# Graph attention on one core: the scores of heads 0 and 1 in one two-bank PSUM tile with one exponential, in place of two one-bank tiles with one exponential each

## The chip, the core and the metric

The kernel runs on one core of a Trainium2 chip. The metric is the device time of one execution in microseconds (us); three runs of the kernel before are given, and one further execution was recorded by the profiler. The engines are named as in the profile: PE is TensorE (PEld its weight loads), DVE is VectorE, ACT is ScalarE, POOL is GpSimd, SP is SyncE, which issues the DMAs. PSUM is the memory that PE writes into; in this kernel it is used as eight banks of 512 float32 columns on 128 partitions.

## What is computed

Two layers of graph attention over 3327 nodes of 128 features. Layer 0 is one softmax over masked cosine scores, a weighted sum, a residual and a layer norm. Layer 1 takes nearly all the time:

```python
q = (x @ Wq.T).reshape(d, n, h)      # d = 128 heads, h = 8 features each
k = (x @ Wk.T).reshape(d, n, h)
v = (x @ Wv.T).reshape(d, n, h)
a = jnp.einsum('dnh,dmh->dnm', q, k) * scale
a = a + spatial_encoding + edge_encoding     # both are adj, so a + 2 adj
a = jax.nn.softmax(a, axis=2)
out = jnp.einsum('dnm,dmh->dnh', a, v)
```

So there are 128 heads of 8 features, each with a full 3327 by 3327 score matrix and a full softmax with its row maximum. A last projection, a residual and a layer norm follow.

## The kernel before, in words

The first two stages (layer 0, and the projections with their transposes to DRAM) end at about 1740 us of the profile. The change lies in the third stage, the attention of layer 1, which runs from there to about 16380 us. The final projection follows.

**Units.** The work of the attention is cut into units of four heads and one block of queries. There are nine blocks: eight of three tiles (384 queries), and a last one of two tiles (256 queries). With 32 groups of four heads this makes 288 units, 256 of 384 queries and 32 of 256. A unit runs over 26 tiles of 128 keys, and each of these is a *step*: 7488 steps in all, 6656 with 384 query columns and 832 with 256.

**What a step does.** The order of the instructions on PE, ACT, DVE and POOL is the order in which the loop at L705 writes them (`manual_schedule`); nothing reorders them. In each step, in this order:

1. PE writes the shift (the negative row maximum, in three bf16 parts) of heads 2 and 3 into the tile `eb`, which has two banks (`shifts`, L592).
2. PE makes the score products for a *later* unit's row maxima, and DVE reduces them (`max_pair`: two heads in two banks, reduced at L515 or L526; `max_single`: one head in one bank, reduced at L536 or L540; the products are L500). A step has one pair and one single. One of them stands here, the other at point 5. When the pair is of heads 0 and 1 it comes here, else the single does. Both have a single buffer, so the products of a step wait for DVE's reduction of the same kind of the step before. In the last block only every second step has a pair.
3. PE adds the scores of heads 2 and 3 to `eb` (`scores`, L598). ACT takes the exponential of both heads from the two banks in one instruction (L724) into `pb`, and POOL multiplies `pb` with the exponential of twice the adjacency (L725).
4. PE writes the shift of heads 0 and 1 into two tiles `ea` of one bank each (L592).
5. PE makes the other of the two products for the row maxima.
6. PE adds the scores of heads 0 and 1 (L598), and then twice the adjacency (`add_adj`, L579): four matmuls for head 0, then four for head 1, on four groups of 32 output columns.
7. ACT takes the exponentials of `ea`, one instruction for head 0 and one for head 1 (L754), into the two halves of `pa`.
8. PE multiplies the `pa` and `pb` of two steps earlier with the values and adds to `acc` (`weigh`, L609).

In some steps of each unit there is more: at key tiles 22 to 24 (of 26) PE turns the next unit's shift in the unused columns 384 to 511 of head 0's `ea` bank and ACT copies it out (L565, L745); at key tile 20 the same place takes the finished output of the unit before (L627, L639); at key tile 1 ACT copies `acc` (L620).

**PSUM.** The eight banks are all used: two by `ea` (a pool of two one-bank buffers), two by `eb`, two by the pair of row-maximum products, one by the single, one by `acc`. Each step therefore takes the same two `ea` buffers, and the shift of a head in the next step waits for the exponential that read that head's buffer.

Of the kernel before, what the change touches and what calls it, by code (L numbers as in the profile page):

```python
# [9 lines left out]
F32 = mybir.dt.float32  # L10
F32R = mybir.dt.float32r
BF16 = mybir.dt.bfloat16
AF = mybir.ActivationFunctionType
ALU = mybir.AluOpType
AX = mybir.AxisListType
PSUM = bass.MemoryType.PSUM
DRAM = bass.MemoryType.DRAM

P = 128
# [26 lines left out]
def gnn_two_layers(  # L46
# [11 lines left out]
    nc = tc.nc  # L58
# [328 lines left out]
    with ExitStack() as at:  # L387
# [1 line left out]
        keys = at.enter_context(tc.tile_pool(name="at_k", bufs=3))  # L389
        pp = at.enter_context(tc.tile_pool(name="at_p", bufs=4))  # L390
        sm = at.enter_context(tc.tile_pool(name="at_sm", bufs=2))
        ps_a = at.enter_context(tc.tile_pool(name="at_a", bufs=2, space=PSUM))
        ps_b = at.enter_context(tc.tile_pool(name="at_b", bufs=1, space=PSUM))
        ps_m = at.enter_context(tc.tile_pool(name="at_m", bufs=1, space=PSUM))
        ps_o = at.enter_context(tc.tile_pool(name="at_o", bufs=1, space=PSUM))
# [29 lines left out]
        def load_adj_tile(b, j):  # L425
            w = width(b)
            nc.sync.dma_start(aT[:, j, :w], aT_s[b][:, j, :w])

        def exp_adj_tile(b, j):
            w = width(b)  # L430
            nc.scalar.activation(eT[:, j, :w], aT[:, j, :w], AF.Exp, scale=2.0)
# [4 lines left out]
        def load_unit(i):  # L436
            b, g = units[i]
            u = Unit()
            u.i, u.b, u.g = i, b, g
            u.nq = width(b)  # L440
            u.nt = u.nq // P

            u.kx = keys.tile([P, NP], F32R, name="kx")
            u.qx = keys.tile([P, QB], F32R, name="qx")
            kx, qx = u.kx.bitcast(F32), u.qx.bitcast(F32)
            for c in range(2):
                nc.sync.dma_start(
                    kx.rearrange("(y c) n -> c y n", c=2)[c],
                    kp_s[4 * g : 4 * g + 4].rearrange("d f r n -> (d f r) n"),
                )  # L450
                for r in range(2):
                    nc.sync.dma_start(
                        qx.rearrange("(y r c) n -> r c y n", r=2, c=2)[r, c, :, : u.nq],
                        qp_s[4 * g : 4 * g + 4, :, c, b * QB : b * QB + u.nq].rearrange(
                            "d f n -> (d f) n"
                        ),
                    )
            u.vt = keys.tile([P, 4, T, H + 1], F32, name="vt")
            nc.sync.dma_start(u.vt, vt_s[g])
            if g % 2 == 0:  # L460
                load_unit.mx = sm.tile([P, 2, 4, QT, 7], F32, name="mx")
            u.mx_both = load_unit.mx
            u.mx = u.mx_both[:, g % 2]
            u.cx = sm.tile([P, QB], BF16, name="cx")
            return u
# [96 lines left out]
        def shift_turn(u, q, dst, start):  # L562
            for h in range(4):
                r = slice(32 * h, 32 * h + 32)
                nc.tensor.matmul(  # L565
                    dst[r],
                    parts[u.i % 2][:, q, h],
                    unit,
                    start=start,
                    stop=True,  # L570
                    tile_position=(0, 32 * h),
                    skip_group_check=True,
                )
# [90 lines left out]
        with tc.manual_schedule(  # L664
            engines={
                mybir.EngineType.PE,
                mybir.EngineType.Activation,
                mybir.EngineType.DVE,
                mybir.EngineType.Pool,
            }  # L670
        ):
            us = {0: load_unit(0), 1: load_unit(1)}
            steps = {}

            def max_step(k):

                i, j = divmod(k, 2 * T)
                if 2 * i >= NU:
                    return None
                if j == 0:  # L680
                    steps[i] = max_steps(2 * i, 2 * i + 1)
                return steps[i][j]

            def new_a():
                return [ps_a.tile([P, 512], F32, name="ea") for _ in range(2)]

            for j in range(T):
                load_adj_tile(0, j)
            for k in range(T + AHEAD):
                pair, single = max_step(k)  # L690
                max_pair(*pair)
                max_single(*single)
                if k == T:
                    shift_parts(us[0])
            e = ps_b.tile([P, 2, 512], F32, name="eb")
            for q in range(QT):
                shift_turn(us[0], q, e[:, 0, q * P : (q + 1) * P], True)
            nc.scalar.copy(us[0].cx, e[:, 0, :QB])
            for j in range(T):
                exp_adj_tile(0, j)  # L700

            todo = []
            turn = []
            done = None
            for s in range(NU * T + LAG):  # L705
                i, j = divmod(s, T)
                u = us.get(i)
                if u is not None:
                    if j == 2 and i + 2 < NU:
                        us[i + 2] = load_unit(i + 2)  # L710
                    k = s + T + AHEAD
                    pair, single = max_step(k) or (None, None)
                    early = pair is not None and pair[1] == (0, 1)

                    e_b = ps_b.tile([P, 2, 512], F32, name="eb")
                    b01 = [e_b[:, x] for x in range(2)]
                    shifts(u, b01, (2, 3))
                    if early:
                        max_pair(*pair)
                    elif single is not None:  # L720
                        max_single(*single)
                    scores(u, j, b01, (2, 3), True)
                    pt_b = pp.tile([P, 2, QB], F32, name="pb")
                    nc.scalar.activation(pt_b[:, :, : u.nq], e_b[:, :, : u.nq], AF.Exp)  # L724
                    nc.gpsimd.tensor_tensor(  # L725
                        pt_b[:, :, : u.nq],
                        pt_b[:, :, : u.nq],
                        eT[:, j, : u.nq].unsqueeze(1).to_broadcast([P, 2, u.nq]),
                        ALU.mult,
                    )  # L730
                    e_a = new_a()
                    shifts(u, e_a, (0, 1))
                    if early:
                        max_single(*single)
                    elif pair is not None:
                        max_pair(*pair)
                    scores(u, j, e_a, (0, 1), False)
                    free = e_a[0][:, QB:]
                    x = us.get(i + 1)
                    copies = []  # L740
                    q = j - (T - 4)
                    if x is not None and 0 <= q < x.nt:
                        shift_turn(x, q, free, False)
                        copies.append(
                            lambda: nc.scalar.copy(x.cx[:, q * P : (q + 1) * P], free)  # L745
                        )
                    if j == T - 6 and done is not None:
                        values_turn(done, free, False)
                        copies.append(lambda: finish(done, free))
                    pt_a = pp.tile([P, 2, QB], F32, name="pa")  # L750
                    for h, e in enumerate(e_a):
                        add_adj(e, u, j)
                    for h, e in enumerate(e_a):
                        nc.scalar.activation(pt_a[:, h, : u.nq], e[:, : u.nq], AF.Exp)  # L754
                    for f in copies:
                        f()
                    todo.append((u, j, (pt_a, pt_b)))

                    if k % (2 * T) in (T, 2 * T - 1):
                        v = us.get(k // (2 * T) * 2 + (k % (2 * T) > T))  # L760
                        if v is not None:
                            shift_parts(v)
                if s >= LAG:
                    w = todo.pop(0)
                    weigh(*w)
                    if w[1] == T - 1:
                        take(w[0])
                        done = us.pop(w[0].i)

                if turn and turn[0][0] <= s:  # L770
                    exp_adj_tile(*turn.pop(0)[1:])
                if u is not None and i + 1 < NU and units[i + 1][0] != u.b:
                    load_adj_tile(u.b + 1, j)
                    turn.append((s + 5, u.b + 1, j))
            e = ps_b.tile([P, 2, 512], F32, name="eb")
            values_turn(done, e[:, 0], True)
            finish(done, e[:, 0])
# [73 lines left out]
```

## Time and profile before

| | |
|---|---|
| three runs, median | 16488.67 us (16487.55 to 16496.15) |
| the profiled execution's own time | 16497.24 us |
| its span, from the first to the last instruction | 16495.5 us |
| attention stage, 384-column units | about 1741 to 15099 us |
| attention stage, 256-column units | about 15099 to 16378 us |
| exponential of heads 2 and 3, 128x768 (L724) | 6656 of 811 ns |
| exponential of head 0 or 1, 128x384 (L754) | 13312 of 490 ns |
| the same with 512 and 256 columns | 832 of 598 ns, 1664 of 383 ns |
| mean granted TensorE clock | 0.971 over the span, 1.00 in the attention |

The profile gives each instruction a start and a duration. In the timeline view a row merges instructions of the same kind that stand next to each other: the first column is the start of the first, the second the time from there to the end of the last, and "x2" how many there are. The text in brackets is the time that the engine sat idle before it, and whom it waited for. Matmuls run in several groups of rows or columns of the array at once, and their ends are modelled. A PE that looks busy throughout may therefore still be waiting in its queue; this is seen only by comparing the start of a matmul with the end of the instruction on another engine that it waits for.

### The profile page before, as it was taken

The page shows a single profiled execution, that of the slowest core. Times are in us where ns is not written, and L with a number is a line of the kernel's source. Part 1 is how long each engine was busy: PE and PEld are TensorE (multiplying, and loading weights), DVE is VectorE, ACT ScalarE, POOL GpSimd, SP SyncE. Part 2 cuts the span into 40 slices and gives each one's busy share as a digit, 9 for nine tenths or more (in the row PEclk, how much of TensorE's full clock was granted, in tenths as well). Part 3 has the DMA queues.
Part 4 walks back from the last instruction along what each step waited for, and adds up shares of the span by engine and source line. Part 5 has one row for each costly group of instructions (what it writes and reads, how often), then busy time and mean ns, then how long its engine had stood idle before and what let it go on. Part 6 is the DMA issues. An engine that isn't in the chain of part 4 may idle for free.

```text
span 16495.5 us, 506265 instructions
## 1 busy us (share of the span) xinstructions
PE 15510.9 (94%) x217532; PEld 6894.2 (42%) x217532; DVE 14320.0 (87%) x16017; ACT 12381.3 (75%) x24535; POOL 14030.4 (85%) x9088
## 2 busy tenths in 40 slices
PE   4462899999999999999999999999999999999999
PEld 3341344444444444444444444444444444444555
DVE  8862899999999999999999999999999999998775
ACT  1220688888888888888888888888888888888776
POOL 3314699999999999999999999999999999999886
PEclk7786899999999999999999999999999999999999
DMA  1127111111111111111111111111111111111112
GB/s 66 63 114 286 65 49 49 49 55 49 49 49 55 48 45 49 55 49 49 49 55 49 49 49 54 45 49 49 55 49 49 49 55 49 49 47 54 65 60 69
DMA packets 415019, 988.86 MB, mean 60 GB/s; under 512 B 192224, under 2 KB 312544, under 8 KB 367200
## 3 DMA queue, kind: packets, MB, share of 16 engines
q1 hardware_dynamic: 412768, 956.46, 17.0%
q8 instruction: 1704, 27.92, 0.7%
q14 instruction: 547, 4.48, 0.1%
HBM read 808.05 MB, written 148.24 MB: 58 GB/s over the span
## 4 chain that ended last, share of the span: by engine, by line
PE 89%; DVE 4%; issue 3%; DMA 2%; POOL 1%; ACT 1%; SPq 0%; DVEq 0%; ACTq 0%; POOLq 0%
PE acc L609 28%; PE ea L579 19%; PE m L500 14%; PE eb L592 12%; PE ea L592 9%; PE ea L598 2%; PE eb L598 2%; DVE mx L515 1%; PE ea L565 1%; DVE s L273 1%; PE av L187 1%; POOL low L359 1%; PE ea L627 1%; DVE mx L536 1%; PE sc L170 0%
## 5 line engine op out<-in xcount | busy, mean ns | idle before, releaser
L725 POOL TENSOR_TENSOR pb<-pb,eT 128x768 f32<-128x768 f32 (+1 forms) x7488 | 13176.2, 1765 | 1102.7 <-ACT pb L724 868.1
L515 DVE TENSOR_REDUCE mx<-m 128x2 f32<-128x1024 f32 x6784 | 8272.9, 1219 | 518.3 <-PE eb L598 277.3
L724 ACT ACTIVATE pb<-eb 128x768 f32<-128x768 f32 (+1 forms) x7488 | 5896.2, 787 | 2506.1 <-PE eb L598 1765.1
L500 PE MATMUL m<-kx,qx 32*128 32x512 f32 (+1 forms) x23296 | 6784.1, 471 | 160.9 <-DMA vt<-vt_s 117.5
L754 ACT ACTIVATE pa<-ea 128x384 f32<-128x384 f32 (+1 forms) x14976 | 6339.6, 478 | 55.2 <-PE ea L579 42.3
L609 PE MATMUL acc<-pb,vt 128*9 128x384 f32 (+1 forms) x29952 | 5903.5, 474 | 0.1
L609 PE MATMUL acc<-pa,vt 128*9 128x384 f32 (+1 forms) x29952 | 5900.7, 474 | 0.0
L536 DVE TENSOR_REDUCE mx<-m 128x1 f32<-128x512 f32 x6400 | 4378.9, 684 | 692.1 <-PE m L500 317.9
L592 PEld LDWEIGHTS <-one 3*128 3x128 bf16 x29952 | 1508.8, 91 | 5565.7 <-issue 4663.3
L579 PE MATMUL ea<-aT,two 128*32 128x384 bf16 (+1 forms) x59904 | 3715.8, 325 | 0.0
L598 PE MATMUL ea<-qx,kx 32*128 32x384 f32 (+1 forms) x14976 | 3444.3, 437 | 0.0
L598 PE MATMUL eb<-qx,kx 32*128 32x384 f32 (+1 forms) x14976 | 3437.2, 451 | 0.0
L592 PE MATMUL ea<-cx,one 3*128 3x384 bf16 (+1 forms) x14976 | 3294.8, 322 | 2.2
L500 PEld LDWEIGHTS m<-kx,qx 32*128 32x128 f32 x23296 | 2815.8, 182 | 525.4 <-issue 117.8
L592 PE MATMUL eb<-cx,one 3*128 3x384 bf16 (+1 forms) x14976 | 2462.4, 326 | 11.1 <-ACT pb L724 10.4
L609 PEld LDWEIGHTS acc<-pa,vt 128*9 128x9 f32 x29952 | 1410.9, 91 | 786.9 <-issue 0.3
L579 PEld LDWEIGHTS <-two 128*32 128x32 bf16 x59904 | 946.2, 95 | 1418.7 <-issue 1278.2
L598 PEld LDWEIGHTS eb<-qx,kx 32*128 32x128 f32 x14976 | 1461.2, 189 | 0.0
L598 PEld LDWEIGHTS ea<-qx,kx 32*128 32x128 f32 x14976 | 1431.2, 182 | 8.4 <-issue 4.5
L609 PEld LDWEIGHTS acc<-pb,vt 128*9 128x9 f32 x29952 | 1417.8, 91 | 0.6 <-POOL pb L725 0.6
L540 DVE TENSOR_REDUCE mx<-m 128x2 f32<-128x512 f32 x1088 | 748.0, 688 | 96.2 <-PE eb L598 44.8
L187 PE MATMUL av<-xs,pt 128*128 128x128 f32 x1352 | 223.4, 330 | 476.2 <-DVE rden L292 310.4
(113 smaller groups left out, 5245.1 us busy)
## 6 DMA issues: line engine op xcount, KB each, us to landing
kx<-kp_s SPq DMA_DIRECT2D x576, 832.0 KB, 4.7
vt<-vt_s SPq DMA_DIRECT2D x288, 468.0 KB, 4.9
qx<-qp_s SPq DMA_DIRECT2D x1024, 48.0 KB, 5.0
raw<-in_adj_dram SPq DMA_DIRECT2D x25, 1663.5 KB, 6.3
aT_s<-aT SPq DMA_DIRECT2D x8, 2496.0 KB, 9.2
aT<-aT_s SPq DMA_DIRECT2D x208, 96.0 KB, 1.9
vt_s<-vals SPq DMA_DIRECT2D x8, 1872.0 KB
q_s<-row SPq DMA_DIRECT2D x26, 512.0 KB, 2.6
```

The costliest lines, as they stand in the source:

```text
L187: nc.tensor.matmul(acc, pt[:, i * P : (i + 1) * P], value(t), start=(t == 0), stop=(t == T - 1))
L500: nc.tensor.matmul(dst, u.qx[rows(a), q * P : (q + 1) * P], u.kx[rows(a), k0:k1], start=True, stop=True,)
L515: nc.vector.tensor_reduce(u.mx[:, h, qs[0], c], m, axis=AX.X, op=ALU.max)
L536: nc.vector.tensor_reduce(u.mx[:, a, qs[0], c : c + 1], m, axis=AX.X, op=ALU.max)
L540: nc.vector.tensor_reduce(u.mx[:, a, qs[0] : qs[1] + 1, c], m.rearrange("p (q k) -> p q k", q=2), axis=AX.X, op=ALU.max,)
L579: nc.tensor.matmul(e[r, : u.nq], two[:, r], aT[:, j, : u.nq], start=False, stop=True, tile_position=(0, 32 * c), skip_group_check=True,)
L592: nc.tensor.matmul(e[:, : u.nq], one[r], u.cx[r, : u.nq], start=True, stop=False, skip_group_check=True)
L598: nc.tensor.matmul(e[:, : u.nq], u.kx[rows(a), j * P : (j + 1) * P], u.qx[rows(a), : u.nq], start=False, stop=stop, skip_group_check=True,)
L609: nc.tensor.matmul(acc[32 * h : 32 * h + H + 1, : u.nq], u.vt[:, h, j], pts[h // 2][:, h % 2, : u.nq], start=(j == 0), stop=(j == T - 1), ...
L724: nc.scalar.activation(pt_b[:, :, : u.nq], e_b[:, :, : u.nq], AF.Exp)
L725: nc.gpsimd.tensor_tensor(pt_b[:, :, : u.nq], pt_b[:, :, : u.nq], eT[:, j, : u.nq].unsqueeze(1).to_broadcast([P, 2, u.nq]), ALU.mult,)
L754: nc.scalar.activation(pt_a[:, h, : u.nq], e[:, : u.nq], AF.Exp)
```

## The change

The pool of `ea` gets one buffer in place of two, and its tile has two banks in place of one. The two heads' score tiles are the two halves of this tile. The two exponentials become one instruction over both halves. `free`, the unused columns of head 0's bank, is in the same place as before. In the built instruction streams the number and the order of all other instructions are the same. On PE the shift of head 0 now waits for the one exponential of the step before, and the shift of head 1, which waited for its own head's, has no wait left; on ACT the one exponential waits for the last of the eight `add_adj` matmuls, where before the first exponential waited for the fourth and the second for the eighth.

```diff
-        ps_a = at.enter_context(tc.tile_pool(name="at_a", bufs=2, space=PSUM))
+        ps_a = at.enter_context(tc.tile_pool(name="at_a", bufs=1, space=PSUM))
...
-            def new_a():
-                return [ps_a.tile([P, 512], F32, name="ea") for _ in range(2)]
-
...
-                    e_a = new_a()
+                    ea = ps_a.tile([P, 2, 512], F32, name="ea")
+                    e_a = [ea[:, x] for x in range(2)]
                     shifts(u, e_a, (0, 1))
...
                     pt_a = pp.tile([P, 2, QB], F32, name="pa")
-                    for h, e in enumerate(e_a):
+                    for e in e_a:
                         add_adj(e, u, j)
-                    for h, e in enumerate(e_a):
-                        nc.scalar.activation(pt_a[:, h, : u.nq], e[:, : u.nq], AF.Exp)
+                    nc.scalar.activation(pt_a[:, :, : u.nq], ea[:, :, : u.nq], AF.Exp)
```

## The prediction

> **What bounds the kernel now.** I read the page first, for the busy shares and the costliest groups, then the timeline of two steady steps of a 384-column unit and of two steps of a 256-column unit, since the page's shares hide which wait ends last.
>
> ```profile
> PE 15510.9 (94%) x217532; PEld 6894.2 (42%) x217532; DVE 14320.0 (87%) x16017; ACT 12381.3 (75%) x24535; POOL 14030.4 (85%) x9088
> ...
> L515 DVE TENSOR_REDUCE mx<-m 128x2 f32<-128x1024 f32 x6784 | 8272.9, 1219 | 518.3 <-PE eb L598 277.3
> ...
> L754 ACT ACTIVATE pa<-ea 128x384 f32<-128x384 f32 (+1 forms) x14976 | 6339.6, 478 | 55.2 <-PE ea L579 42.3
> ```
>
> PE never looks idle and ACT has a quarter of the span free: by these shares alone, shortening ACT is worth nothing. But PE's idleness does not show when its queue waits, so I compare starts with ends. In the timeline of a 384-column unit, two successive steps:
>
> ```profile
> 9072.84 0.87 ACT L754 ACTIVATE pa<-ea 128x384 f32<-128x384 f32 x2
> ...
> 9073.46 0.33 PE L592 MATMUL eb<-cx,one 3*128 3x384 bf16 x2
> ...
> 9073.81 0.34 PE L592 MATMUL ea<-cx,one 3*128 3x384 bf16 x2
> ...
> 9074.01 1.23 DVE L515 TENSOR_REDUCE mx<-m 128x2 f32<-128x1024 f32 x1 [0.24 <-PE eb L598]
> 9074.11 0.81 ACT L724 ACTIVATE pb<-eb 128x768 f32<-128x768 f32 x1 [0.41 <-PE eb L598]
> 9074.26 0.51 PE L579 MATMUL ea<-aT,two 128*32 128x384 bf16 x8
> ...
> 9074.82 0.87 ACT L754 ACTIVATE pa<-ea 128x384 f32<-128x384 f32 x2
> ...
> 9075.15 0.68 DVE L536 TENSOR_REDUCE mx<-m 128x1 f32<-128x512 f32 x1
> ...
> 9075.69 0.37 PE L592 MATMUL ea<-cx,one 3*128 3x384 bf16 x2
> ...
> 9075.89 0.50 PE L500 MATMUL m<-kx,qx 32*128 32x512 f32 x1
> ...
> 9076.32 0.51 PE L579 MATMUL ea<-aT,two 128*32 128x384 bf16 x8
> ...
> 9076.78 0.87 ACT L754 ACTIVATE pa<-ea 128x384 f32<-128x384 f32 x2
> ...
> 9077.41 0.33 PE L592 MATMUL eb<-cx,one 3*128 3x384 bf16 x2
> ```
>
> The two steps take 9077.41 - 9073.46 = 3.95 us, 1.97 each. There is a loop of DVE and PE with just this length. From the shift of `eb` (9073.46) to the pair's reduction (9074.01) is 0.55; pair and single reduce back to back until 9075.15 + 0.68 = 9075.83, 1.82; the next step's single product starts 0.06 later (9075.89), because its only buffer has just come free; adds start 0.43 after it (9076.32); the shift of `eb` two steps on comes 1.09 later. 0.55 + 1.82 + 0.06 + 0.43 + 1.09 = 3.95. **DVE's reductions and the way back through PE set the pace of the 384-column units**, and no exponential is in that loop. Counted over the first 6000 steps of the trace, one of the two products starts 0.06 behind its reduction in 82% of them.
>
> ACT is close behind. Its loop runs through `ea`: shift, adds, exponentials, shift. At 9075.69 the two exponentials end (9074.82 + 0.87), and the row of the `ea` shift that starts there spans 0.37 instead of 0.34, which puts its second matmul some 0.05 after that end: PE waited for ACT. But the single product that follows waits for DVE until 9075.89 anyway, so this wait is covered.
>
> In the 256-column units DVE has half the pairs, and the same comparison gives another bound:
>
> ```profile
> 15505.00 0.28 PE L592 MATMUL eb<-cx,one 3*128 3x256 bf16 x2
> ...
> 15505.83 0.40 PE L579 MATMUL ea<-aT,two 128*32 128x256 bf16 x8
> ...
> 15506.24 0.66 ACT L754 ACTIVATE pa<-ea 128x256 f32<-128x256 f32 x2
> ...
> 15506.60 0.28 PE L592 MATMUL eb<-cx,one 3*128 3x256 bf16 x2
> ...
> 15506.67 0.55 PE L592 MATMUL ea<-cx,one 3*128 3x256 bf16 x2
> ...
> 15507.27 0.40 PE L579 MATMUL ea<-aT,two 128*32 128x256 bf16 x8
> ...
> 15507.73 0.66 ACT L754 ACTIVATE pa<-ea 128x256 f32<-128x256 f32 x2
> ```
>
> The exponentials end at 15506.90; the `ea` row that follows spans 0.55 for two matmuls of some 0.28, so the second starts at about 15506.95, 0.05 after them. Here **ACT's loop through `ea` is the bound**.
>
> **The change part by part.**
>
> *One exponential for two.* Two 128x384 take 0.87 from the first start to the last end; one 128x768 from two banks is L724 as it stands, 0.81. That is 0.06 less ACT time per step, 0.06 x 6656 = 400 us in all, and 0.66 - 0.60 = 0.06 on the 832 small steps. All of it lies beside the DVE loop in the large units, so it is worth nothing as such.
>
> The Trainium skill (ScalarE: Activation LUTs, What ACT_TABLE_LOAD costs) gives an ACTIVATE a fixed 186 ns plus 0.833 ns per column, with 93 ns overlapped back to back. By that rule merging would take 93 ns off each step, 0.70 ms over 7488 steps if ACT set the pace, and the time would be some 15,800 us. The rows above have 0.06, and ACT does not set it.
>
> *The later start.* Before, head 0's exponential starts 0.11 us after its own four adds where nothing else holds it (112 ns is the median of such steps in the trace; in the timeline the first four end at about 9076.32 + 0.34, and 9076.78 follows, when the eight still run until 9076.32 + 0.51 = 9076.83). The merged one needs all eight. No row shows this wait; the nearest is the same 0.11 behind the eighth add. So at the first step shown it starts at 9074.26 + 0.51 + 0.11 = 9074.88 instead of 9074.82 and ends at 9075.69, as now. At the second it starts at 9076.94 instead of 9076.78 and ends at 9077.75 instead of 9077.65: 0.10 later. **The change delays the release of `ea`, although it shortens ACT.** Behind it on PE's queue, everything of the step waits.
>
> The Trainium skill (PSUM — Partial Sum Buffer, Summary: rules for kernel authors) says to aim at a different bank when reading PSUM while matmuls run. That speaks against this change: two separate banks let head 0 be read while head 1 is written, which the 9076.78 row shows for 0.05 us.
>
> *What the delay costs in the large units.* The new loop through `ea` is: shift to adds 0.44 at the least (9073.81 to 9074.26), eight adds 0.51, wait 0.11, exponential 0.81, release 0.05: 1.92. The DVE loop needs 1.97 on average, so 0.05 of slack is left per step. It bites only where steps alternate between short and long, as here: 9075.34 to 9077.41 is 2.07 and the one before 1.88, below 1.92. Since the DVE loop ties each step to the one after the next, the short step can grow to 1.92 and the long one shrink to 2.02 at no cost, except once, when the pattern is entered, about 0.045 us per unit. 256 units x 0.045 = 12 us. Ends: 0 (absorbed in the slower steps at the unit's end) to 0.09 per unit, 23 us.
>
> *What it costs in the small units.* First step: adds end 15506.23, merged start 15506.34, plus 0.60 is 15506.94 against 15506.90: 0.04 to 0.05 later, on the bounding loop. Second step: adds end 15507.67, start 15507.78, end 15508.38 against 15508.39: nothing. 0.049 x 416 pairs of steps = 20 us. Ends: 0, and 0.05 on each of the 832, 42 us.
>
> *The rest.* PE drops one wait per step and head 0's shift waits longer than before; it had been ready 0.4 us before its turn, and the loop above counts it with head 1's. The copies out of `free` (272 ns, 3 per unit) come behind an exponential that ends up to 0.10 later; the next use of ACT is L724, before which ACT now sits idle 0.4 us, and that hides it. `weigh` reads `pa` two steps later. No DMA moves, and SP and POOL get the same instructions in the same order.
>
> **Sum.** 16497.2 (the profiled execution's own time, 1.7 over its span) + 12 + 20 = 16529. That execution lies 8.6 us above the median of the three runs, 16488.7; timed runs should so give 16521, +0.19%.
>
> **Rivals.** (1) *Markedly slower: the loop through `ea` becomes the bound everywhere.* Place: shift, adds, exponential, shift. It has 0.05 us of slack at 1.92; from there each further 0.01 costs up to 0.01 x 6656 = 67 us. If the merged exponential started 0.06 us later than I count (the wait for the eighth add is no row of before), half of it would be eaten by slack: 0.02 x 6656 = 130 on the large units and 0.06 x 832 = 50 on the small ones beyond the forecast, 16,700. For it: matmul ends are modelled. Against: 0.11 holds wherever head 0 waits for its adds. 20%. (2) *Faster: ACT's chain L724, L754, L754 sets the pace.* For it: `ea` follows the exponentials by 0.05 in 30% of those 6000 steps. If it were the bound over two steps, 0.06 per pair of steps comes off: 0.03 x 6656 = 200 us, 16,290. Against: in just those steps the adds end too late for the merged start to gain (9074.88, above). 8%. (3) *Nothing measurable changes*: both delays are absorbed, 16,489, as the small steps' loop finds slack that I do not see. 6%.
>
> **Chances.** Forecast 66%, with its own range 16,490 to 16,555 from the ends above. A measurement of this kernel can tell about 0.2% from no change, which is 16,521.7, so the forecast lies on that line: of its 66 I put 36 within and 30 above. Faster 8, within 36 + 6 = 42, slower 30 + 20 = 50. The range that leaves two in ten out: from 16,475 to 16,650.
>
> **What will show it.** The row of `pa` should be one 128x768 with 0.81, started 0.11 behind the last add; large steps that alternate 1.92 and 2.02 in place of 1.88 and 2.07; single products still 0.06 behind DVE's single. In the small units two steps should take 3.08 in place of 3.03. I am wrong if the single product no longer follows DVE by 0.06 (rival 1: then `ea`'s shift follows the exponential by 0.05 in every step), or if the two-step time of the large units falls below 3.93.

## The result, and the profile after

| | before | changed |
|---|---|---|
| median of the runs | 16488.39 us (16487.55 to 16496.15, 4 runs) | 16630.01 us (16626.7 to 16630.85, 4 runs) |
| span of the profiled execution | 16495.5 us | 16628.2 us |
| 384-column units, from their first step's shift to the first one of the 256-column units | 13358.4 us | 13462.3 us |
| 256-column units, from their first step's shift to their last's | 1278.5 us | 1306.5 us |

The ratio is 1.0084, 95% interval 1.0067 to 1.0102: 142 us slower. Of the 132.7 us between the spans, 103.9 lie in the large units and 28.0 in the small ones; the stages around them differ by 1 us.

The page of the changed kernel, the lines that answer to those shown of before:

```profile
PE 15583.1 (94%) x217532; PEld 6981.7 (42%) x217532; DVE 14314.6 (86%) x16017; ACT 12396.5 (75%) x17047; POOL 14050.3 (84%) x9088
...
L515 DVE TENSOR_REDUCE mx<-m 128x2 f32<-128x1024 f32 x6784 | 8271.3, 1219 | 563.0 <-PE eb L598 296.9
...
L751 ACT ACTIVATE pa<-ea 128x768 f32<-128x768 f32 (+1 forms) x7488 | 5897.5, 788 | 618.6 <-PE ea L579 268.8
```

The exponentials of heads 0 and 1 are busy 442 us less (6339.6 before), and ACT's idle time just before them has grown from 55.2 to 618.6 us, most of what a releaser is named for being a wait for the adds of L579. ACT as a whole is no less busy, since the exponential of heads 0 and 1 now mostly starts after L721 has ended, where before it overlapped L724's end by up to 0.11 us.

In the steady steps of the large units the timeline of the changed kernel shows what was forecast:

```profile
9130.17 0.34 PE L592 MATMUL ea<-cx,one 3*128 3x384 bf16 x2
...
9130.62 0.51 PE L579 MATMUL ea<-aT,two 128*32 128x384 bf16 x8
...
9131.25 0.81 ACT L751 ACTIVATE pa<-ea 128x768 f32<-128x768 f32 x1
...
9131.47 0.68 DVE L536 TENSOR_REDUCE mx<-m 128x1 f32<-128x512 f32 x1
...
9132.11 0.34 PE L592 MATMUL ea<-cx,one 3*128 3x384 bf16 x2
...
9132.20 0.49 PE L500 MATMUL m<-kx,qx 32*128 32x512 f32 x1
```

From one `ea` shift to the next are 0.45 to the adds, 0.51 for them, 0.12 to the exponential, 0.81, and 0.05 to the shift: 1.94 us. The product for the row maximum still starts 0.05 behind the end of DVE's single (9131.47 + 0.68 = 9132.15). DVE still sets the pace here. Over the key tiles 8 to 19 of all units, that product starts 0.05 behind DVE's single in 89% of the steps (93% before), and two steps take 3.932 us in the median, 3.935 before.

The time is lost elsewhere. Measured from one start of the exponential of heads 2 and 3 to the next, medians over the units of 384 columns with an even number, by key tile:

| key tile | before, ns | changed, ns |
|---|---|---|
| 8 to 19, alternating | 1876 to 1880 and 2060 to 2064 | 1922 to 1946 and 2018 to 1986 |
| 21 | 1946 | 2059 |
| 22 | 2056 | 2040 |
| 23 | 2023 | 2133 |
| 24 | 2023 | 2133 |
| 25 | 1970 | 2079 |

In the mean over all 256 units, key tiles 21, 23, 24 and 25 are 0.42 us longer in sum; all other 22 tiles of a unit together are 0.01 us shorter (mean unit 52.137 us before, 52.543 changed). 0.41 x 256 is the 104 us. In key tiles 20 and 22 to 24 ACT copies something out of the unused columns of `ea`. The kernel before, in one of these steps:

```profile
9100.98 0.87 ACT L754 ACTIVATE pa<-ea 128x384 f32<-128x384 f32 x2
...
9101.74 0.27 ACT L745 CAST cx<-ea 128x128 bf16<-128x128 f32 x1
...
9101.95 0.42 PE L592 MATMUL ea<-cx,one 3*128 3x384 bf16 x2
...
9102.56 0.50 PE L579 MATMUL ea<-aT,two 128*32 128x384 bf16 x8
...
9103.00 0.87 ACT L754 ACTIVATE pa<-ea 128x384 f32<-128x384 f32 x2
```

The copy ends at 9102.01. The row of the `ea` shift spans 0.42 us for two matmuls of 0.33, so its second starts at about 9102.04 to 9102.06: behind the copy. In the trace this second shift starts 50 to 53 ns after the end of the copy, behind all 1022 copies of the large units. So **these steps were held by the loop through `ea` before the change already**, not by DVE: 0.94 from the second shift to the exponentials (9102.06 to 9103.00), 0.87 for them, the copy, which ends 0.16 later, and 0.05 to the next such shift. From exponential to exponential it is 2.02 us. The first of the two shifts, head 0's, starts 0.02 to 0.11 us before the copy's end, although by the program the copy reads head 0's tile. In the run below that turns the order of the adds, the first shift stands 0.05 behind the *second* exponential in these steps. It looks as if behind a copy the two buffers are taken in the order in which they come free; no view shows the buffer. The changed kernel:

```profile
9157.51 0.81 ACT L751 ACTIVATE pa<-ea 128x768 f32<-128x768 f32 x1 [0.21 <-PE ea L579]
...
9158.22 0.26 ACT L743 CAST cx<-ea 128x128 bf16<-128x128 f32 x1
...
9158.53 0.34 PE L592 MATMUL ea<-cx,one 3*128 3x384 bf16 x2
...
9159.03 0.50 PE L579 MATMUL ea<-aT,two 128*32 128x384 bf16 x8
...
9159.64 0.81 ACT L751 ACTIVATE pa<-ea 128x768 f32<-128x768 f32 x1 [0.21 <-PE ea L579]
```

The exponential starts 0.11 behind the last add, after 0.21 us of idle ACT; the copy ends at 9158.48, and the shift, here the first of the two, follows 0.05 later. From exponential to exponential are 2.13 us, where the kernel before has 2.02.

### The profile page after: what moved, and what is told of

Read it like the earlier page. It is cut to its first block, busy times and chain, and to the rows that moved or that the text cites. A ratio compares the mean times of both kernels' runs of the same rounds, so it can differ in the third digit from the quotient of the medians.

```text
span 16628.2 us, 498777 instructions
## 1 busy us (share of the span) xinstructions
PE 15583.1 (94%) x217532; PEld 6981.7 (42%) x217532; DVE 14314.6 (86%) x16017; ACT 12396.5 (75%) x17047; POOL 14050.3 (84%) x9088
## 4 chain that ended last, share of the span: by engine, by line
PE 87%; DVE 4%; issue 3%; ACT 2%; DMA 2%; POOL 1%; SPq 0%; ACTq 0%; DVEq 0%; POOLq 0%
PE acc L609 27%; PE ea L579 19%; PE m L500 14%; PE eb L592 11%; PE ea L592 10%; PE ea L598 2%; ACT pa L751 1%; DVE mx L515 1%; PE ea L565 1%; DVE s L273 1%; PE eb L598 1%; PE av L187 1%; POOL low L359 1%; PE ea L627 1%; DVE mx L536 1%
## 5 line engine op out<-in xcount | busy, mean ns | idle before, releaser
L721 ACT ACTIVATE pb<-eb 128x768 f32<-128x768 f32 (+1 forms) x7488 | 5900.0, 788 | 2059.4 <-PE eb L598 1423.6
L500 PE MATMUL m<-kx,qx 32*128 32x512 f32 (+1 forms) x23296 | 6889.5, 472 | 159.9 <-DMA vt<-vt_s 117.6
L751 ACT ACTIVATE pa<-ea 128x768 f32<-128x768 f32 (+1 forms) x7488 | 5897.5, 788 | 618.6 <-PE ea L579 268.8
L592 PEld LDWEIGHTS <-one 3*128 3x128 bf16 x29952 | 1736.8, 91 | 5870.9 <-issue 5034.5
L579 PE MATMUL ea<-aT,two 128*32 128x384 bf16 (+1 forms) x59904 | 3715.3, 325 | 0.0
L592 PE MATMUL ea<-cx,one 3*128 3x384 bf16 (+1 forms) x14976 | 2522.1, 319 | 55.6 <-ACT pa L751 9.1
L579 PEld LDWEIGHTS <-two 128*32 128x32 bf16 x59904 | 946.3, 95 | 1411.0 <-issue 1272.7
```

The costliest lines, as they stand in the source:

```text
L500: nc.tensor.matmul(dst, u.qx[rows(a), q * P : (q + 1) * P], u.kx[rows(a), k0:k1], start=True, stop=True,)
L579: nc.tensor.matmul(e[r, : u.nq], two[:, r], aT[:, j, : u.nq], start=False, stop=True, tile_position=(0, 32 * c), skip_group_check=True,)
L592: nc.tensor.matmul(e[:, : u.nq], one[r], u.cx[r, : u.nq], start=True, stop=False, skip_group_check=True)
L751: nc.scalar.activation(pt_a[:, :, : u.nq], ea[:, :, : u.nq], AF.Exp)
```

## The experiments

**Theory A**, formed from the tables above: the extra time is the loop through `ea`, made some 0.11 us longer by the start behind the eighth add (0.17 later than behind the fourth, less the 0.06 of the shorter exponential). It costs nothing where DVE covers it, and shows where a copy already stands in that loop (four key tiles of each large unit) and in the small units. **Rivals**: B, it is the single buffer and not the instruction; C, the later start costs in every step; D, the copies were hidden before, as the prediction had it; F, PE's own length paces the large units; G, only the copies count. Differences below are taken to the kernel before as it was timed beside each run (16,488.4, 16,495.0 and 16,496.9 us).

**One tile, two exponentials.** The tile and buffer of the change without its instruction:

```diff
-                    nc.scalar.activation(pt_a[:, :, : u.nq], ea[:, :, : u.nq], AF.Exp)
+                    for h, e in enumerate(e_a):
+                        nc.scalar.activation(pt_a[:, h, : u.nq], e[:, : u.nq], AF.Exp)
```

> The changed kernel's two-bank tile with one buffer, but with an exponential per head as before. Theory A (the extra time comes from the one instruction: it starts behind the eighth add and the copies out of the unused columns stand behind it, so in four key tiles of each 384-column unit the shift of ea comes some 0.11 us later): the exponentials and copies end when they did before, so 16,490, within 25 us. Theory B (the one buffer: head 0's shift now waits for what head 1's did): the time stays at 16,630.

Measured: 16,832.8 us, ratio 1.0205 (1.019 to 1.022). Both expectations fail: this is 338 us over before, far slower than the change itself. Its timeline tells why:

```profile
9213.62 0.34 PE L592 MATMUL ea<-cx,one 3*128 3x384 bf16 x2
...
9214.06 0.51 PE L579 MATMUL ea<-aT,two 128*32 128x384 bf16 x8
...
9214.68 0.87 ACT L752 ACTIVATE pa<-ea 128x384 f32<-128x384 f32 x2
...
9215.60 0.34 PE L592 MATMUL ea<-cx,one 3*128 3x384 bf16 x2
```

The first of the two exponentials starts 0.11 behind the *eighth* add (9214.06 + 0.51 = 9214.57), although it reads head 0's half alone. The wait is set by the tile and not by the bank that is read. The loop becomes 0.44 + 0.51 + 0.11 + 0.87 + 0.05 = 1.98 us, over DVE's 1.97, and the steady steps take 1.983 us each, with no alternation left. So the shared tile brings the late start by itself, and **the one exponential wins back 0.06 us of the loop**: 338 us become 142.

**The late start with the two old tiles.** The kernel before, with the adds of head 1 issued ahead of head 0's:

```diff
-                    for h, e in enumerate(e_a):
+                    for e in reversed(e_a):
                         add_adj(e, u, j)
```

> The kernel before with two tiles and two exponentials, but the four adds of head 1 stand before the four of head 0, so that the first exponential waits for all eight adds: the late start alone, without the shorter exponential. The loop of ea grows to 0.44 + 0.51 + 0.11 + 0.87 + 0.05 = 1.98 us, over DVE's 1.97. Theory A: slower than the changed kernel, 16,770 to 16,850, with some 0.17 us more in each of the copies' steps. Theory B or D (the late start is hidden): 16,490.

Measured: 16,789.4 us, ratio 1.0179 (1.0164 to 1.0194), as theory A has it; steady steps take 1.974 to 1.980 us and key tiles 23 and 24 2.19. With two buffers the late start alone costs 295 us, so B falls as the whole cause. The first experiment lies 43 us above this run; there head 0's shift also waits for both exponentials, and B can hold for no more than that.

**The copies moved to another bank.** The turned shift and the finished output go into the unused columns of head 2's `eb` bank, and are copied out behind the exponential of heads 2 and 3; in the changed kernel and in the one before:

```diff
-                    free = e_a[0][:, QB:]
...
                     scores(u, j, b01, (2, 3), True)
+                    free = b01[0][:, QB:]
...
                     nc.scalar.activation(pt_b[:, :, : u.nq], e_b[:, :, : u.nq], AF.Exp)
+                    for f in copies:
+                        f()
...
-                    for f in copies:
-                        f()
```

> The changed kernel, but the turned shifts and the finished output go into the unused columns of head 2's eb bank, and ACT copies them out behind the exponential of heads 2 and 3. Theory A: the four key tiles no longer wait for a copy and fall to about 1.97 us each, about 155 us below the changed kernel, and only the 256-column units' cost stays: 16,460 to 16,480. Theory C (the later start costs in every step, through the loop of ea): at most a few tens of us below the changed kernel, 16,590 or more.

> The kernel before, with the same move of the copies into eb. Theory A: before too the ea shift waited 0.05 us behind the copy in key tiles 21 to 25, at 2.02 us a step; without it the steps fall to DVE's pace, 0.05 us each, about 50 us in all: 16,435, and below the kernel with one exponential and moved copies by the 256-column units' 28 us. Theory D (the copies were hidden before, as the prediction had it): 16,490.

Measured: 16,720.5 us, 1.0137 (1.012 to 1.0154), for the change, and 16,702.0 us, 1.0125 (1.011 to 1.0141), for the kernel before. The kernel before misses both of its expectations by over 200 us, and the change misses theory A's by 240; theory C's bound of 16,590 or more holds it, but C had it below the changed kernel, and it lies 90 us above. The move itself is costly on PE. In a step of key tile 23 of the kernel before, so altered:

```profile
9207.10 0.33 PE L592 MATMUL eb<-cx,one 3*128 3x384 bf16 x2
...
9207.54 0.24 PE L565 MATMUL eb<-unit,parts 128*32 128x128 bf16 x4
...
9207.71 0.33 PE L592 MATMUL ea<-cx,one 3*128 3x384 bf16 x2
...
9208.15 0.51 PE L579 MATMUL ea<-aT,two 128*32 128x384 bf16 x8
...
9208.75 0.90 ACT L756 ACTIVATE pa<-ea 128x384 f32<-128x384 f32 x2
...
9209.24 0.34 PE L592 MATMUL eb<-cx,one 3*128 3x384 bf16 x2
...
9209.85 0.34 PE L592 MATMUL ea<-cx,one 3*128 3x384 bf16 x2
```

The `ea` shift comes 0.61 us after the `eb` shift, against 0.34 to 0.35 in the kernel before. The turn's matmuls use all 128 rows of the array and now stand between groups of 3 and 32 rows that ran side by side. As a test of the copies in `ea` the pair is spoilt one by one, but its difference can be read, since both bear the same cost: 18 us between the kernels, the large units 13543.1 against 13543.4 us, and all of the 18 in the small ones. With the copies out of `ea`, the change costs the large units nothing. For the ordinary steps this says that the later start is free. For the turned steps it says little: there both kernels take 2.13 us, which is PE's own way (0.61 from the `eb` shift to the `ea` shift, 0.44 to the adds, 1.09 to the next `eb` shift), and the exponentials end 0.20 before the next `ea` shift (9209.65 and 9209.85), so that a later start would be covered.

**The copies read something else.** The same instructions in the same order on every engine, but no copy holds `ea`:

```diff
-                            lambda: nc.scalar.copy(x.cx[:, q * P : (q + 1) * P], free)
+                            lambda: nc.scalar.copy(x.cx[:, q * P : (q + 1) * P], ident)
...
-                        copies.append(lambda: finish(done, free))
+                        copies.append(lambda: finish(done, ones))
```

> The changed kernel with the same instructions on every engine, but the copies of the turned shift and of the finished output read a constant in SBUF instead of the unused columns of ea, so that no copy holds the tile; the shifts and outputs are not the reference's. Theory A (in the large units the extra time is the copy behind the exponential): key tiles 21 and 23 to 25 fall from 2.06 to 2.13 us to some 1.97, 26 x 256 steps lose about 0.55 us a unit, 140 us: 16,490. Theory C (the later start costs in every step): within 60 us of the changed kernel, 16,570 or more.

> The kernel before with the same alteration. Theory A: its key tiles 22 to 25 too were held by the copy, at 2.02 to 2.06 us; they fall to 1.97, some 40 to 50 us in all: 16,445, below the changed kernel with this alteration by the 28 us of the 256-column units and some 15 more. Theory D (before, the copies were hidden): 16,490.

Measured: the change 16,527.7 us, 1.0018 (1.0009 to 1.0028); the kernel before 16,466.8 us, 0.9982 (0.9972 to 0.9992). The change costs 61 us in this pair, 34.5 in the large units and 26.7 in the small ones. D falls, as the kernel before gets faster by 30 us (19 of them in the large units); C falls too, as the change loses most of its cost. But 16,528 is 38 us over what A expected, and 16,467 is 22 over it. The pair leaves out the turned shift and the finished output, so it replaces neither kernel. A step of key tile 23 of the changed kernel, so altered, shows what was left out:

```profile
9107.00 0.34 PE L592 MATMUL ea<-cx,one 3*128 3x384 bf16 x2
...
9107.51 0.50 PE L579 MATMUL ea<-aT,two 128*32 128x384 bf16 x8
...
9108.12 0.81 ACT L751 ACTIVATE pa<-ea 128x768 f32<-128x768 f32 x1
...
9108.98 0.34 PE L592 MATMUL ea<-cx,one 3*128 3x384 bf16 x2
```

The shift is no longer behind a copy, but 0.05 behind the exponential. The turn's matmuls (L565) still stand between shift and adds, 0.51 instead of 0.44 us, and the loop takes 1.98 us in these steps with no copy in it, where the kernel before so altered needs 1.92 at the same key tile. So some two thirds of the large units' 104 us (104 - 34.5) go with the copies' hold of the tile. The rest lies in the same part of the unit: between the two kernels so altered, the difference is 0.01 us over key tiles 6 to 19, 0.16 over 20 to 25, and -0.03 over 0 to 5, in the mean over the units. That the turn in the longer loop is its cause is read from these rows and was not tested alone.

**DVE's cover taken away.** Both kernels with shorter single reductions:

```diff
-                nc.vector.tensor_reduce(u.mx[:, a, qs[0], c : c + 1], m, axis=AX.X, op=ALU.max)
+                nc.vector.tensor_reduce(u.mx[:, a, qs[0], c : c + 1], m[:, :128], axis=AX.X, op=ALU.max)
```

> The kernel before, but DVE reduces only the first 128 of a single product's 512 columns, so some row maxima miss keys; the products on PE stay. DVE gets about 0.35 us shorter per step. Theory A (DVE's loop paces the 384-column units, ACT's loop stands close behind): the steps fall until the next loop holds them, to about 1.90 us: 16,030, within 80. Theory F (PE's own length paces them): 16,490.

> The changed kernel with the same shortening of the singles' reductions. Theory A: without DVE's cover the longer loop through ea (0.44 + 0.51 + 0.11 + 0.81 + 0.05 = 1.92 us) shows in every step: 16,330, some 300 us above the kernel before with the same shortening, where the change costs 142 us with the full reductions. Theory G (the exponential's start is not on a loop of its own and only the copies count): the difference stays at about 140 us.

Measured: 16,106.3 us, 0.9763 (0.9748 to 0.9778), for the kernel before, and 16,363.0 us, 0.9918 (0.9903 to 0.9933), for the change. F falls: DVE paced the large units. G falls: the change costs 257 us here against 142 with the full reductions. The changed kernel's loop now stands alone:

```profile
8984.10 0.34 PE L592 MATMUL ea<-cx,one 3*128 3x384 bf16 x2
...
8984.54 0.51 PE L579 MATMUL ea<-aT,two 128*32 128x384 bf16 x8
...
8985.16 0.81 ACT L751 ACTIVATE pa<-ea 128x768 f32<-128x768 f32 x1
...
8986.02 0.34 PE L592 MATMUL ea<-cx,one 3*128 3x384 bf16 x2
```

0.44 + 0.51 + 0.11 + 0.81 + 0.05 = 1.92 us, and the median step is 1.920 to 1.924 us at 18 of the 26 key tiles; the kernel before, so altered, goes on at 1.88 and 1.90 to 1.92 there. Theory A had some 300 us for the difference, a little more than came. This pair leaves out part of the row maxima, so it is no replacement for either kernel. No version that keeps the whole computation and beats the kernel before came out of these runs.

## Why the prediction was right, and where it failed

The range (16,475 to 16,650) held the time, and slower was the likeliest side; the size was off: +32 us against the profiled execution was forecast, +133 us of span came. The forecast's own range, 16,490 to 16,555, did not hold the time. The wider one did because of the chance put on rival 1, and the 104 us came from a term set at nothing: that it held is in good part luck.

*What bounds the kernel*: right for most steps. DVE and PE pace the large units, ACT's loop through `ea` the small ones. It was wrong for the four key tiles behind a copy, which I took for ordinary steps: the 210 ns between the exponentials' end and the next shift there looked like slack, and was the copy.

*One exponential for two*: right, 0.81 for 0.87, and worth nothing as ACT time. The two exponentials on the shared tile show its worth inside the loop.

*The later start*: right, 0.11 behind the eighth add (112 ns in the median of the steady steps), as taken from the nearest row.

*The large units, 12 us*: the loop of 1.92 us and the alternation of 1.92 and 2.02 came as forecast. The cost at the entry of the pattern did not: the 22 other key tiles are 0.01 us a unit shorter, so the term is about -3 us.

*The small units, 20 us*: 28 measured. Two steps take 3.09 us (1.497 and 1.597) where 3.08 was forecast and 3.03 was before. The changed kernel, in two steps:

```profile
15463.15 0.60 ACT L751 ACTIVATE pa<-ea 128x512 f32<-128x512 f32 x1
...
15463.80 0.28 PE L592 MATMUL ea<-cx,one 3*128 3x256 bf16 x2
...
15464.76 0.60 ACT L751 ACTIVATE pa<-ea 128x512 f32<-128x512 f32 x1
...
15465.41 0.28 PE L592 MATMUL ea<-cx,one 3*128 3x256 bf16 x2
...
15466.90 0.28 PE L592 MATMUL ea<-cx,one 3*128 3x256 bf16 x2
```

The `ea` shift starts 0.05 behind the end of the exponential here (15463.75 and 15463.80, 15465.36 and 15465.41), as the prediction had it.

*The rest, nothing*: **this is the step that failed.** It said that the copies out of `free` end later without harm, since "the next use of ACT is L724, before which ACT now sits idle 0.4 us, and that hides it". ACT's next instruction was indeed not late; but the copy also holds the `ea` buffer that PE writes next. One of the next step's two `ea` shifts waited for it before the change, and the first waits for it after, 50 to 53 ns behind its end. The 0.10 to 0.11 us that the exponential loses is passed on there in full: 0.42 us over four key tiles, 107 us over 256 units. The prediction also counted three copies a unit; the finished output's, at key tile 20, is a fourth.

The Trainium skill (PSUM — Partial Sum Buffer, PSUM bank collisions raise a hardware error) has a rule that fits this row: guard PSUM by bank and 32-partition quadrant with semaphores, not by address. In the changed kernel head 0's shift writes columns 0 to 383, the copy reads 384 to 511 of the same bank, and the wait is there. These runs do not tell whether the bank or the whole tile sets it (in the first experiment a wait went by the tile), and none shows what happens without it.

Rival 1, the loop through `ea` as the bound everywhere, was the right mechanism with the wrong place: it decides in the steps whose loop is made longer by a copy or, as far as read from the rows, a turn. Its sign came by half: from key tile 8 to 19 the `ea` shift stands 0.05 behind the exponential in every step, yet the product still follows DVE in 89% of them, so the first half alone does not show this bound. Its price was worked out wrong: a start 0.06 later makes the loop 1.98, which is 0.01 over 1.97, not 0.02. Rival 2 falls with the result, a shorter exponential and a longer time, rival 3 too.

What stays open: the 34.5 us left in the large units without the copies' hold lie in key tiles 20 to 25 and not at the pattern's entry, but no run takes the turn's matmuls alone out of the loop.

## What to carry to other kernels

When two instructions on two tiles are joined into one on a joined tile, compare the start of the joined one (behind the last writer) and its release (behind the last reader) with the two old ones, and lay both into the loop that reuses the buffer; the shorter busy time alone says nothing. Look for every reader of that buffer, also the rare ones in unused columns: a step that occurs in 4 of 26 iterations cost here more than the other 22. An engine at 94% can be waiting in every step; compare the start of its instructions with the end of what releases them, step class by step class.

## What the runs showed of the hardware

- A matmul that waits for ACT starts 0.05 us after ACT's end (50 to 53 ns), one that waits for DVE 0.055 us after it, and an exponential starts 110 to 113 ns after the modelled end of the last matmul that it waits for, in all of these kernels.
- Two 128x384 exponentials back to back overlap by 0.11 us, so that they take 0.87 and not 0.98; one 128x768 takes 0.81.
- Four matmuls of 128 rows between groups that use 3 and 32 rows delayed the next shift by 0.26 us, more than their own row of 0.24 in the timeline; at their old place, next to adds that use 128 rows too, they made the way from shift to adds 0.07 longer.
